# A pre-norm transformer block on one core: down projections of batches 1 to 3 as seven block products

## The chip, the cores and the metric

The kernel runs on 1 core of one Trainium2 chip. The metric is the device time of one execution in microseconds (us), as the median of several runs. The profile is one further execution, recorded by the hardware profiler. Everything is float32. Engines are named as in the profile: PE (TensorE, matrix multiplication), PEld (its weight loads), DVE (VectorE), ACT (ScalarE), POOL (GpSimd) and SP (SyncE, whose queue issues nearly all DMAs).

## The reference

The input holds 4 batches of 512 tokens with 512 features each. With `layernorm` the plain one without scale and shift, the block computes

```
x = x + attention(layernorm(x)) @ Wo        # 32 heads of 16, 8 key/value heads, rope, causal
h = layernorm(x)
x = x + (silu(h @ Wg.T) * (h @ Wu.T)) @ Wd.T    # hidden size 1376
```

The change concerns the last line's product with `Wd`, the down projection: per batch a matrix of 512 tokens by 1376 hidden features times a matrix of 1376 by 512, added to `x`.

## The kernel before

The kernel's program is written out by hand as lists of small steps with an estimated PE cost each. Attention is split in 32 groups (8 per batch, four heads each). While the 8 groups of a batch run, `slot(b, steps)` (L1017) deals steps of other work into the gaps between the attention's visits (`gap`, L1037, in proportion to the summed cost of the list). I call these stretches slot 0 to slot 3; what comes after slot 3 runs without attention beside it and is called the last section.

- Slot 1 holds the output projection of batch 0, its layer norm, its gate and up projections (`ordinary`, L507) and half of its down projection. It also packs combined gate and up weights into DRAM (`packs`, L585; POOL's L603).
- Slot 2 holds the other half of batch 0's down projection, then batch 1: `attended(1)` (output projection, residual add L478, layer norm statistics, and a transposition by DVE and two DMAs, `flipped`, L283, whose rows are called flips), `edge` (the hidden features from 1280 on), `seven` (gate and up projections as seven block products per pair of feature tiles, L647), and half of batch 1's down projection.
- Slot 3 is the same one batch further: rest of batch 1's down projection, batch 2's output projection, layer norm, `edge`, `seven`, and the beginning of its down projection.
- The last section holds the rest of batch 2's down projection and everything of batch 3.

`woven` (L1079) puts the output projection of the next batch (`before`) behind the first four leftover steps of a down projection, then the other leftover steps but one, then a step that emits the outstanding layer norm work (`behind`), then the last one.

The hidden features of a batch stand in `homes[n]` as 11 tiles of 128 features by 512 tokens, the last with 96 features. Tiles 0 to 9 are the `whole` ones. In `seven`, `ended` (L676) finishes a pair of tiles: two products of 128x512 on POOL inside a slot and on DVE outside (L684).

`down(b, n)` (L730) makes, for each of the four 128-token tiles of a batch, 11 products of a stationary 128x128 block of the hidden features with 512 columns of `wd_sb`, all accumulated in one PSUM bank. One DVE instruction (L740) scales by 0.5 and adds the bank to `xr`, and one DMA (L741) stores 256 KB. The down weights are read once into `wd_sb` (L1089). `xr` is a pool of six tiles of 128x512, loaded by L199.

`product_of` (L266) issues one product. Inside slots (`narrow`) it is split in four matmuls of 32 columns of the stationary block (L271); outside it is one matmul (L268). The profile counts each float32 matmul twice, so that a product is 8 records inside a slot and 2 outside. `bank()` (L190) hands out one of three PSUM banks. A list `aside` holds layer norm work that is emitted between steps, two entries per step in the last section.

The SP queue runs in order. Besides the loads of weights it carries what attention needs (`turned_round` L858, `laid_out` L867 and L869), the flips (L290, L292), and the stores of the output.

## Time and profile before

| | us |
|---|---|
| median of 3 runs (857.61 to 859.67) | 858.76 |
| the profiled execution, whole time | 859.25 |
| its span | 857.5 |
| PE busy | 836.6 |
| DVE busy | 533.9 |
| POOL busy | 292.1 |
| ACT busy | 217.1 |

The span is what the profile's times count from; the whole time is 1.7 us longer. Busy times are sums over the span, and the end of a matmul is modelled. Slot 2 ends at about 540 us, slot 3 at about 709 us, and the last section runs from there to the end. In it PE makes the rest of batch 2's down projection and batch 3's output projection (709.5 to 750.1), `edge` (to 755.4), `seven` (755.4 to 816.0) and batch 3's down projection (816.0 to 853.9).

### The profile page before, as it was taken

The page shows a single profiled execution, that of the slowest core. Times are in us where ns is not written, and L with a number is a line of the kernel's source. Part 1 is how long each engine was busy: PE and PEld are TensorE (multiplying, and loading weights), DVE is VectorE, ACT ScalarE, POOL GpSimd, SP SyncE. Part 2 cuts the span into 40 slices and gives each one's busy share as a digit, 9 for nine tenths or more (in the row PEclk, how much of TensorE's full clock was granted, in tenths as well). Part 3 has the DMA queues.
Part 4 walks back from the last instruction along what each step waited for, and adds up shares of the span by engine and source line. Part 5 has one row for each costly group of instructions (what it writes and reads, how often), then busy time and mean ns, then how long its engine had stood idle before and what let it go on. Part 6 is the DMA issues. An engine that isn't in the chain of part 4 may idle for free.

```text
span 857.5 us, 26970 instructions
## 1 busy us (share of the span) xinstructions
PE 836.6 (98%) x11446; PEld 420.5 (49%) x11446; DVE 533.9 (62%) x1593; ACT 217.1 (25%) x296; POOL 292.1 (34%) x418
## 2 busy tenths in 40 slices
PE   6999999999999999999999999999999999999998
PEld 5654453544333335333655553335555544498843
DVE  7887778878555554457777774586777523356610
ACT  1034444422222222221233332222333320011100
POOL 4565564773444344222233332232243330000000
PEclk9999999999999999999999999999999999999999
DMA  7533304003765742335134320214332402545300
GB/s 252 122 98 77 90 16 80 15 3 71 234 182 165 203 135 78 127 155 113 59 92 120 102 89 15 65 27 114 104 108 89 118 28 66 108 136 161 105 12 37
DMA packets 133463, 85.10 MB, mean 99 GB/s; under 512 B 59264, under 2 KB 120320, under 8 KB 133088
## 3 DMA queue, kind: packets, MB, share of 16 engines
q1 hardware_dynamic: 133056, 77.62, 32.4%
q10 hardware_dynamic: 288, 5.77, 1.7%
q8 instruction: 90, 1.47, 0.7%
q14 instruction: 29, 0.24, 0.1%
HBM read 64.56 MB, written 22.54 MB: 102 GB/s over the span
## 4 chain that ended last, share of the span: by engine, by line
PE 81%; DVE 10%; POOL 3%; DMA 2%; issue 2%; ACT 1%; SPq 1%; POOLq 0%; DVEq 0%; ACTq 0%
PE mm L271 38%; PE mm L268 18%; PE sc L771 12%; PE av L899 6%; DVE junk L817 6%; PE sc L784 4%; POOL e L877 2%; PE mm L553 2%; ACT e L872 1%; PE mm L545 1%; DVE st L218 1%; DVE rot L330 1%; DMA xa<-in_x 1%; POOL qa L756 1%; DMA shared<-in_wg 1%
## 5 line engine op out<-in xcount | busy, mean ns | idle before, releaser
L817 DVE CUSTOM_DVE_ANT_0 junk<-sc,mask 128x128 f32<-128x128 f32 (+3 forms) x512 | 251.0, 490 | 140.5 <-PE sc L784 80.3
L872 ACT ACTIVATE e<-sc 128x1024 f32<-128x1024 f32 (+1 forms) x192 | 165.4, 881 | 376.5 <-PE sc L784 307.8
L271 PE MATMUL mm<-xnT,shared 128*32 128x256 f32 (+1 forms) x3520 | 243.9, 420 | 1.4 <-DMA shared<-in_wg 1.4
L877 POOL TENSOR_SCALAR_AFFINE_SELECT e<-e 128x512 f32<-128x512 f32 (+2 forms) x192 | 106.2, 563 | 264.5 <-ACT e L872 261.3
L271 PEld LDWEIGHTS mm<-xnT,shared 128*32 128x32 f32 x3520 | 116.9, 110 | 112.1 <-issue 63.6
L771 PE MATMUL sc<-home,qa 32*64 32x512 f32 (+6 forms) x2048 | 157.9, 421 | 5.5 <-DVE low L817 3.1
L784 PE MATMUL sc<-qa,home 32*64 32x512 f32 (+6 forms) x2048 | 152.2, 427 | 2.2 <-DVE low L817 1.6
L771 PEld LDWEIGHTS sc<-home,qa 32*64 32x64 f32 x2048 | 67.3, 131 | 94.2 <-issue 31.1
L271 PE MATMUL mm<-wd_sb,home 128*32 128x512 f32 (+1 forms) x808 | 94.0, 595 | 0.0
L899 PE MATMUL av<-e,home 128*32 128x512 f32 (+3 forms) x1024 | 82.3, 437 | 1.5 <-POOL e L877 1.1
L268 PE MATMUL mm<-xnT,shared 128*128 128x256 f32 x360 | 80.6, 384 | 0.0
L268 PEld LDWEIGHTS mm<-xnT,shared 128*128 128x128 f32 x360 | 68.7, 192 | 11.7 <-issue 2.2
L784 PEld LDWEIGHTS sc<-qa,home 32*64 32x64 f32 x2048 | 58.7, 130 | 26.5 <-issue 8.7
L268 PE MATMUL mm<-wd_sb,home 128*128 128x512 f32 (+1 forms) x150 | 65.0, 593 | 0.0
L740 DVE SCALAR_TENSOR_TENSOR xr<-mm,xr 128x512 f32<-128x512 f32 x16 | 11.0, 686 | 71.5 <-PE mm L268 54.9
L899 PEld LDWEIGHTS av<-e,home 128*32 128x32 f32 x1024 | 30.9, 109 | 46.7 <-issue 35.5
L271 PEld LDWEIGHTS mm<-wd_sb,home 128*32 128x32 f32 (+1 forms) x808 | 26.9, 110 | 50.8 <-issue 48.9
L268 PEld LDWEIGHTS mm<-wd_sb,home 128*128 128x128 f32 (+1 forms) x150 | 28.4, 190 | 35.8 <-issue 35.8
L271 PE MATMUL mm<-wo_sb,cx 128*32 128x512 f32 x384 | 44.9, 595 | 0.0
L817 DVE DVE_READ_ACCUMULATOR2_ANT low<- 128x1 f32 x512 | 42.3, 83 | 0.0
L221 POOL TENSOR_TENSOR rstd<-rstd,neghalf 128x1 f32<-128x1 f32 x32 | 20.4, 639 | 61.4 <-DVE rstd L220 60.9
L923 POOL TENSOR_TENSOR inv<-us,inverse 128x256 f32<-128x256 f32 x32 | 20.9, 654 | 49.1 <-DVE inverse L916 47.9
(108 smaller groups left out, 669.5 us busy)
## 6 DMA issues: line engine op xcount, KB each, us to landing
shared<-packed SPq DMA_DIRECT2D x90, 256.0 KB
flip<-u SPq DMA_DIRECT2D x88, 64.0 KB
packed<-xnT SPq DMA_DIRECT2D x10, 512.0 KB
xnT<-flip SPq DMA_DIRECT2D x18, 256.0 KB
xr<-in_x SPq DMA_DIRECT2D x16, 256.0 KB
out<-xr SPq DMA_DIRECT2D x16, 256.0 KB
shared<-packed SPq DMA_DIRECT2D x30, 128.0 KB
xa<-in_x SPq DMA_DIRECT2D x12, 256.0 KB
```

Source lines behind the costliest of these rows:

```text
L221: nc.gpsimd.tensor_tensor(rstd, rstd, neghalf, ALU.pow)
L268: nc.tensor.matmul(out, lhsT=lhsT, rhs=rhs, start=start, stop=stop)
L271: nc.tensor.matmul(out[c : c + 32], lhsT=lhsT[:, c : c + 32], rhs=rhs, start=start, stop=stop)
L553: nc.tensor.matmul(ps[96:P, ts(q, P)], lhsT=rest_w[:, a, kq, 32 * q : 32 * q + 32], rhs=xnTs[0][:, kq, most:], start=kq == 0, stop=kq == N ...
L740: nc.vector.scalar_tensor_tensor(xr[b, i], py[i], 0.5, xr[b, i], ALU.mult, ALU.add)
L771: nc.tensor.matmul(dst[at : at + 64, :n], lhsT=qa[g][rows_of(r), q : q + 64], rhs=keys_of(g)[rows_of(r), :n], start=True, stop=True,)
L784: nc.tensor.matmul(dst[at : at + 64, first_q:], lhsT=keys_of(g)[rows_of(r), k : k + 64], rhs=qa[g][rows_of(r), P * j + first_q :], start=True,
L817: nc.vector.tensor_tensor_reduce(out=junk[:, :n], in0=src, in1=mask[:, T - n : T] if i else mask[:, T:], scale=-1.0, scalar=BIG, op0=ALU.a ...
L872: nc.scalar.activation(dst, src, AF.Exp, scale=1.0 / math.sqrt(DH))
L877: nc.gpsimd.affine_select(out=e[rows, heads, c : c + P], in_=e[rows, heads, c : c + P], compare_op=ALU.is_ge, fill=0.0, base=base, pattern ...
L899: nc.tensor.matmul(av[32 * r : 32 * r + 32, P * j :], lhsT=v[:, j, 4 * (m // 2) + r, DH * (1 - hf) : DH * (3 - hf)], rhs=e[:, r, c : c + n ...
L923: nc.gpsimd.tensor_tensor(us[m][:, :, hf, :], turned[0][:, :, hf, :], by, ALU.mult)
```

## The change

For batches 1 to 3 the ten whole feature tiles are taken as five pairs. For each pair, the hidden block (256 features by 512 tokens) and the weight block (256 features by 512 outputs) are cut into 2 by 2 blocks, and the product is made from seven block products instead of eight. Each of the seven products P1 to P7 is accumulated over the five pairs in a PSUM bank of its own, and DVE then adds the banks to the quadrants of the output. The 96 last features are multiplied as before, inside the banks of P2, P4 and P3 and in a bank called E.

- The combined hidden blocks are made by POOL (`hidden_sum`, four instructions of 128x256 per pair; two inside `seven`, two while P2 and P4 run).
- The combined weight blocks are made once by POOL in slot 2 (`differ`, 20 instructions) and stored to DRAM (five stores of 512 KB).
- The weight blocks of each stage are read as one DMA of 640 KB (`load_stage`), into places that stood free: two for batch 1, more for batches 2 and 3 (`PLACE`).
- `xr` becomes four fixed tiles of two rows each (`rows`).
- Per batch there are 39 steps of two products (256 columns each) instead of 20 steps; the first 17 stand where the first half stood, the next five where `woven` had four leftover steps, and the remaining 17 behind the output projection of the next batch.

```diff
-    xr = {}
+    rows = [const.tile([P, 2, D], F32, name=f"rows{n}") for n in range(3)] + [homes[3][:, 8:10, :]]
+    ROWS = {0: (0, 1), 1: (2, 0), 2: (1, 3), 3: (2, 0)}
+    xr = {(b, i): rows[ROWS[b][i // 2]][:, i % 2, :] for b in range(B) for i in range(NT)}
...
     def load_xr(b, i):
-        t = work.tile([P, D], F32, tag="xr", name="xr", bufs=6)
-        nc.sync.dma_start(out=t, in_=x[b, ts(i, P), :])
-        xr[b, i] = t
+        nc.sync.dma_start(out=xr[b, i], in_=x[b, ts(i, P), :])
...
-        steps = [step for u in range(whole) for step in unit(u)]
+        steps = []
+        for u in range(whole):
+            steps += unit(u)
+            for which in range(2 if u > 1 and u % 2 == 0 else 0):
+                steps.insert(len(steps) - 4 + 3 * which, after(lambda u=u, w=which: hidden_sum(n, u // 2 - 1, w)))
...
-        return [ends[0], t[0], ends[1], t[1], ends[2], t[2], ends[3], t[3], *steps[:12], after(moved), *steps[12:]]
+        last = [after(lambda w=w: hidden_sum(n, whole // 2 - 1, w)) for w in range(2)]
+        steps[12:12] = [after(moved)]
+        for cut, step in zip((44, 50, 56, 62, 66, 70), blocks):
+            steps.insert(cut, after(step))
+        return [ends[0], t[0], ends[1], t[1], ends[2], t[2], ends[3], t[3], *steps, *last]
...
+    def hidden_of(n, parity, half, p):
+        return homes[n][:, 2 * p + parity, halved_d * half : halved_d * (half + 1)]
+
+    def hidden_sum(n, p, which):
+        a11, a12, a21, a22 = (hidden_of(n, k, h, p) for h in range(2) for k in range(2))
+        s = third[:, p]
+        to, one, two, op = (
+            (s, a21, a22, ALU.add),
+            (a21, a11, a21, ALU.subtract),
+            (s, s, a11, ALU.subtract),
+            (a12, a12, s, ALU.subtract),
+        )[which]
+        nc.gpsimd.tensor_tensor(to, one, two, op)
+
+    def differ(p):
+        t = xnTs[1][:, 2 * (p % 2) : 2 * (p % 2) + 2, :].rearrange("p k t -> p (k t)")
+        t = t.rearrange("p (s d) -> p s d", s=4)
+        b11, b12, b21, b22 = (wd_sb[:, 2 * p + k, halved_d * h :][:, :halved_d] for k in range(2) for h in range(2))
+        def combine(which):
+            to, one, two = ((0, b12, b11), (1, b22, b12), (2, b22, t[:, 0]), (3, b21, t[:, 2]))[which]
+            nc.gpsimd.tensor_tensor(t[:, to], one, two, ALU.subtract)
+        def store():
+            nc.sync.dma_start(out=differences[:, p], in_=t)
...
+    STAGES = (("P5", None, 0), ("P2", (0, 0), (1, 0)), ("P4", (1, 0), 3), ("P7", None, 1),
+        ("P1", None, (0, 0)), ("P6", None, 2), ("E", (1, 1), None), ("P3", (0, 1), (1, 1)))
+    PLACE = {1: (0, 1, 0, 1, 0, 1, 0), 2: (1, 0, 1, 0, 2, 3, 4), 3: (5, 0, 1, 2, 3, 4, 5)}
...
+        lefts = {
+            "P5": lambda p: third[:, p],
+            "P6": lambda p: third[:, p],
+            "P2": lambda p: hidden_of(n, 1, 0, p),
+            "P3": lambda p: hidden_of(n, 1, 0, p),
+            "P1": lambda p: hidden_of(n, 0, 0, p),
+            "P7": lambda p: hidden_of(n, 0, 1, p),
+            "P4": lambda p: hidden_of(n, 1, 1, p),
+        }
...
+        def add(half, d, name):
+            at = quadrant(half, d)
+            nc.vector.scalar_tensor_tensor(at, two(banks[name]), 0.5, at, ALU.mult, ALU.add)
...
+        ends = {
+            "P5": [lambda: add(0, 1, "P5"), lambda: add(1, 1, "P5")],
+            "P2": [lambda: add(0, 0, "P2")],
+            "P4": [lambda: add(1, 0, "P4")],
+            "P7": [lambda: add(1, 0, "P7"), lambda: add(1, 1, "P7")],
+            "P1": [keep, lambda: final(0, 0, "P1")],
+            "P6": [joined, lambda: final(1, 0, "P6"), lambda: add(1, 1, "P6"), lambda: add(0, 1, "P6")],
+            "E": [lambda: final(1, 1, "E")],
+            "P3": [lambda: final(0, 1, "P3")] if b < B - 1 else [],
+        }
...
+            inner = [*(range(5) if name != "E" else ()), *([None] if edge else ())]
+            todo = [(i, p, p == inner[0], p == inner[-1]) for i in range(2) for p in inner]
...
+                steps.append((0.86, lambda args=args: step(*args)))
+                if at == 0 and k is not None and (b == 1 and 1 <= k < 6 or b == 2 and 1 <= k < 3):
+                    steps.append(after(lambda k=k: load_stage(b, k + 1)))
+                if at == 0 and name == "P2" and b == 3:
+                    steps.append(after(lambda: load_stage(3, 6)))
+                if name in ("P2", "P4") and at < 10:
+                    which = 2 if name == "P2" else 3
+                    steps.append(after(lambda p=at // 2, which=which: hidden_sum(n, p, which)))
...
+    asides = []
+    for p in range(5):
+        combine, store = differ(p)
+        asides += [(0.5 + 5.2 * p + 1.2 * n, lambda n=n, combine=combine: combine(n)) for n in range(4)]
+        asides += [(7.0 + 5.2 * p, store)]
...
-    slot(2, [after(restored), *woven(before, others, behind), *seven(1, 0), *tiles[:cut]])
+    opening = timed([*others[:4], *before, *others[4:-1], *behind, others[-1]], asides)
+    now, opener, rest = split(1, 0)
+    slot(2, [after(restored), *opening, *seven(1, 0, stages_of(1, (0, 1))), *now])
...
-    slot(3, [*woven(before, others, behind), *seven(2, 2), *tiles[:cut]])
+    woven = [*opener, *before, *rest[:-1], *behind, rest[-1]]
+    now, opener, rest = split(2, 2)
+    slot(3, [*woven, *seven(2, 2, stages_of(2, (0, 1))), *now])
...
-    for cost, step in [*woven(before, tiles[cut:], behind), *seven(3, 0), *down(3, 0)]:
+    loads = [after(step) for step in stages_of(2, (4, 5, 6))]
+    woven = [*opener, *loads, *before, *rest[:-1], *behind, rest[-1]]
+    for cost, step in [*woven, *seven(3, 0, stages_of(3, range(6))), *down7(3, 0)]:
```

In `step` (inside `down7`, not shown) each step first emits one of the DVE additions that the stages before it owe, then its two products; those of P4, P7 and P3 are emitted at the end of the stage. `keep` is two ACT copies of P1's bank, `joined` two DVE additions of 128x256, `final` an addition and a store of 256 KB. P3 of batch 3 is added and stored by 128x256 halves.

More of the change, by code (lines that the diff above doesn't have):

```diff
@@ L491, in begin @@
         def begin():
-            if (b, 0) not in xr:
+            if b > 0:
                 for i in range(NT):
@@ L645, in sums_of, with seven @@
         nc.vector.tensor_tensor(one, two, by, ALU.subtract)
-    def seven(b, n):
+    def seven(b, n, blocks):
         x, home = xnTs[0], homes[n]
@@ new lines, in seven @@
+        steps[12:12] = [after(moved)]
+        for cut, step in zip((44, 50, 56, 62, 66, 70), blocks):
+            steps.insert(cut, after(step))
+        return [ends[0], t[0], ends[1], t[1], ends[2], t[2], ends[3], t[3], *steps, *last]
+    halved_d = 2 * P
+    pieces = homes[3].rearrange("p f t -> p (f t)")[:, : 8 * T]
+    ring = [pieces[:, 1280 * s : 1280 * (s + 1)] for s in range(2)]
+    ring += [homes[1].rearrange("p f t -> p (f t)")[:, 1280 * s : 1280 * (s + 1)] for s in range(4)]
+    ring = [t.rearrange("p (j d) -> p j d", j=5) for t in ring]
@@ new lines, in preln_block_kernel @@
+    third = pieces[:, 2560 : 2560 + 1280].rearrange("p (j t) -> p j t", j=5)
+    differences = dram.tile([P, 5, 4, halved_d], F32, name="differences")
+    def hidden_of(n, parity, half, p):
[10 more added lines that the diff above has]
+        nc.gpsimd.tensor_tensor(to, one, two, op)
@@ new lines, in differ @@
+    def differ(p):
[7 more added lines that the diff above has]
+            nc.sync.dma_start(out=differences[:, p], in_=t)
+        return combine, store
@@ new lines, in preln_block_kernel, with load_stage @@
+    STAGES = (
+        ("P5", None, 0),
+        ("P2", (0, 0), (1, 0)),
+        ("P4", (1, 0), 3),
+        ("P7", None, 1),
+        ("P1", None, (0, 0)),
+        ("P6", None, 2),
+        ("E", (1, 1), None),
+        ("P3", (0, 1), (1, 1)),
+    )
+    NAMES = [name for name, _, _ in STAGES if name != "E"]
+    PLACE = {1: (0, 1, 0, 1, 0, 1, 0), 2: (1, 0, 1, 0, 2, 3, 4), 3: (5, 0, 1, 2, 3, 4, 5)}
+    def load_stage(b, k):
+        src = next(src for name, _, src in STAGES if name == NAMES[k])
+        if isinstance(src, int):
+            view = differences[:, :, src, :]
+        else:
+            parity, half = src
+            view = wd[: whole * P, halved_d * half : halved_d * (half + 1)]
+            view = view.rearrange("(j a p) d -> a p j d", a=2, p=P)[parity]
+        nc.sync.dma_start(out=ring[PLACE[b][k]], in_=view)
@@ new lines, in down7, with quadrant, two, give @@
+    def down7(b, n):
+        banks, owed, steps = {}, deque(), []
+        lefts = {
[7 more added lines that the diff above has]
+        }
+        def quadrant(half, d):
+            return rows[ROWS[b][half]][:, :, halved_d * d : halved_d * (d + 1)]
+        def two(t):
+            return t.rearrange("p (i d) -> p i d", i=2)
+        def add(half, d, name):
+            at = quadrant(half, d)
+            nc.vector.scalar_tensor_tensor(at, two(banks[name]), 0.5, at, ALU.mult, ALU.add)
+        def give(half, d):
+            to = out[b, halved_d * half : halved_d * (half + 1), halved_d * d : halved_d * (d + 1)]
+            nc.sync.dma_start(out=to.rearrange("(i p) d -> p i d", p=P), in_=quadrant(half, d))
+        kept = (rope_sb[:, 2 * NK * 96 : 2 * T], pieces[:, 15 * halved_d :])
+        def keep():
+            for i in range(2):
+                nc.scalar.copy(kept[i], banks["P1"][:, ts(i, halved_d)])
+        def joined():
+            for i in range(2):
+                at = banks["P6"][:, ts(i, halved_d)]
+                nc.vector.tensor_tensor(at, at, kept[i], ALU.add)
+        def final(half, d, name):
+            add(half, d, name)
+            give(half, d)
+        ends = {
[8 more added lines that the diff above has]
+        }
+        def product(name, i, left, right, first, last):
+            product_of(banks[name][:, ts(i, halved_d)], left[:, ts(i, P)], right, first, last)
+        def step(name, products, first, final_step):
+            if first:
+                banks[name] = bank()
+            if owed:
+                owed.popleft()()
+            for i, p, start, stop in products:
+                if p is None:
+                    half, d = edges[name]
+                    left = homes[n][: FF - whole * P, whole, halved_d * half : halved_d * (half + 1)]
+                    right = wd_sb[: FF - whole * P, whole, halved_d * d : halved_d * (d + 1)]
+                else:
+                    left, right = lefts[name](p), ring[PLACE[b][NAMES.index(name)]][:, p]
+                product(name, i, left, right, start, stop)
+                if stop and b == B - 1 and name == "P3":
+                    at = quadrant(0, 1)[:, i]
+                    nc.vector.scalar_tensor_tensor(at, two(banks[name])[:, i], 0.5, at, ALU.mult, ALU.add)
+                    nc.sync.dma_start(out=out[b, ts(i, P), halved_d:], in_=at)
+            if final_step:
+                owed.extend(ends[name])
+                while owed and (name in ("P4", "P7", "P3") or owed[0] in (keep, joined)):
+                    owed.popleft()()
+        edges = {name: edge for name, edge, _ in STAGES}
+        for name, edge, _ in STAGES:
+            inner = [*(range(5) if name != "E" else ()), *([None] if edge else ())]
+            todo = [(i, p, p == inner[0], p == inner[-1]) for i in range(2) for p in inner]
+            k = NAMES.index(name) if name != "E" else None
+            for at in range(0, len(todo), 2):
+                args = name, todo[at : at + 2], at == 0, at + 2 == len(todo)
+                steps.append((0.86, lambda args=args: step(*args)))
[6 more added lines that the diff above has]
+                    steps.append(after(lambda p=at // 2, which=which: hidden_sum(n, p, which)))
+        return steps
@@ L1077, in slot @@
             step()
-    def woven(before, others, behind):
-        return [*others[:4], *before, *others[4:-1], *behind, others[-1]]
     def spilled():
@@ L1138, in preln_block_kernel, with split, stages_of @@
     slot(1, [*start1, *timed(layer, asides)])
+    asides = []
[3 more added lines that the diff above has]
+        asides += [(7.0 + 5.2 * p, store)]
+    def split(b, n):
+        steps = down7(b, n)
+        at = [[i for i, (cost, _) in enumerate(steps) if cost][k] for k in (17, 22)]
+        return steps[: at[0]], steps[at[0] : at[1]], steps[at[1] :]
+    def stages_of(b, ks):
+        return [lambda k=k: load_stage(b, k) for k in ks]
     before, behind = attended(1)
-    tiles, others = list(down(1, 0)), tiles[cut:]
-    cut = len(tiles) // 2
-    slot(2, [after(restored), *woven(before, others, behind), *seven(1, 0), *tiles[:cut]])
+    others = tiles[cut:]
+    opening = timed([*others[:4], *before, *others[4:-1], *behind, others[-1]], asides)
+    now, opener, rest = split(1, 0)
+    slot(2, [after(restored), *opening, *seven(1, 0, stages_of(1, (0, 1))), *now])
     before, behind = attended(2)
-    tiles, others = list(down(2, 2)), tiles[cut:]
-    cut -= 4
-    slot(3, [*woven(before, others, behind), *seven(2, 2), *tiles[:cut]])
+    woven = [*opener, *before, *rest[:-1], *behind, rest[-1]]
+    now, opener, rest = split(2, 2)
+    slot(3, [*woven, *seven(2, 2, stages_of(2, (0, 1))), *now])
     before, behind = attended(3)
-    for cost, step in [*woven(before, tiles[cut:], behind), *seven(3, 0), *down(3, 0)]:
+    loads = [after(step) for step in stages_of(2, (4, 5, 6))]
+    woven = [*opener, *loads, *before, *rest[:-1], *behind, rest[-1]]
+    for cost, step in [*woven, *seven(3, 0, stages_of(3, range(6))), *down7(3, 0)]:
         step()
```

## The prediction

> **What bounds the kernel now.** I read the page first: its busy times, the granted clock and the chain that ended last.

> ```profile
> PE 836.6 (98%) x11446; PEld 420.5 (49%) x11446; DVE 533.9 (62%) x1593; ACT 217.1 (25%) x296; POOL 292.1 (34%) x418
> ...
> PEclk9999999999999999999999999999999999999999
> ...
> PE 81%; DVE 10%; POOL 3%; DMA 2%; issue 2%; ACT 1%; SPq 1%; POOLq 0%; DVEq 0%; ACTq 0%
> ```

> PE is busy 98% of the span at full clock and carries 81% of the chain. Of PE's 21 us of idle time all but about 1 lie in the first 215 us and behind its last matmul (the table of windows). So in the stretches that the change touches, PE time taken away is time won, and a wait of PE is time lost.

> Second, the groups with shapes kept apart, for counts and for POOL's prices.

> ```profile
> L271 PE MATMUL mm<-wd_sb,home 128*32 128x512 f32 x736 | 86.4, 595 | 0.0
> ...
> L268 PE MATMUL mm<-wd_sb,home 128*128 128x512 f32 x136 | 59.6, 593 | 0.0
> ...
> L603 POOL TENSOR_TENSOR xnT<-xnT 128x256 f32<-128x256 f32 x40 | 29.2, 731 | 4.9 <-DMA xnT<-in_wg 2.1 <-DMA xnT<-in_wu 0.7
> ...
> L684 POOL TENSOR_TENSOR home<-home,u 128x512 f32<-128x512 f32 x20 | 25.2, 1283 | 24.8 <-DVE u L720 24.6
> ...
> L740 DVE SCALAR_TENSOR_TENSOR xr<-mm,xr 128x512 f32<-128x512 f32 x16 | 11.0, 686 | 71.5 <-PE mm L268 54.9 <-PE mm L271 16.6
> ```

> The means overlap each other in pipelined matmuls, so they are no price. For that I took bursts from the timeline of PE (start, length, count):

> ```profile
> 508.95 1.93 PE L271 MATMUL mm<-xnT,shared 128*32 128x256 f32 x32
> ...
> 657.77 3.66 PE L271 MATMUL mm<-xnT,shared 128*32 128x256 f32 x64
> ...
> 567.07 3.64 PE L271 MATMUL mm<-wo_sb,cx 128*32 128x512 f32 x32
> 571.58 1.92 PE L271 MATMUL mm<-wo_sb,cx 128*32 128x512 f32 x16
> ...
> 764.83 51.32 PE L268 MATMUL mm<-xnT,shared 128*128 128x256 f32 x237
> 815.98 37.95 PE L268 MATMUL mm<-wd_sb,home 128*128 128x512 f32 x88
> ```

> In a slot 16 more records of 512 columns (two products) take 1.72 us, so 0.86 a product; 32 more of 256 columns (four products) take 1.73, so 0.4325. In the last section it is 37.95/44 = 0.8625 and 51.32 x 2/237 = 0.433. Half the columns cost half: smaller products are not punished, though each needs a weight load of its own.

> **The change, part by part.** *Matmuls.* Before, batches 1 and 2 have 44 + 13 products of 512 columns in slots, and 31 + 44 stand in the last section. After, 78 + 34 of 256 columns stand in slots, and 44 + 78 in the last section. Slots: 57 x 0.86 = 49.0 against 112 x 0.4325 = 48.4. Last section: 75 x 0.8625 = 64.7 against 122 x 0.433 = 52.8. Sum: -12.5 us. Nearly all of it appears in the last section, since 17 of 39 steps stand in slot 3 where 6 of 20 did.

> *The end.* The last instructions before:

> ```profile
> 816.18 0.69 DVE L720 TENSOR_TENSOR u<-mm,u 128x512 f32<-128x512 f32 x1 [0.58 <-PE mm L268]
> 816.91 1.29 DVE L684 TENSOR_TENSOR home<-home,u 128x512 f32<-128x512 f32 x2
> ...
> 853.96 0.69 DVE L740 SCALAR_TENSOR_TENSOR xr<-mm,xr 128x512 f32<-128x512 f32 x1 [8.76 <-PE mm L268]
> ```

> The last addition becomes 128x256 (0.42, row of L712), and its store 128 KB instead of 256: at the 320 GB/s of the busiest slices 0.4 us less. Together -0.6 (0 to -0.8).

> *The wait for the combined hidden block.* The first two lines above also price the hand-over. P5 begins where tile 0 of the down projection began, but its fifth product needs the sum of the two blocks that the last unit of `seven` has just finished; before, those tiles were the ninth and tenth of eleven, 6.9 us in. Batch 3: from the last matmul of `seven` (816.0) DVE needs until 818.2, POOL's sum 0.73 and hand-overs 0.2, so the block is ready after 3.1 us. PE has four products until then, 1.7 us: it waits 1.4. Batches 1 and 2: both products of L684 run on POOL (2.5 us), behind L720, which DVE reaches 0.2 us late behind its transposition; ready after 0.9 + 2.5 + 0.8 + 0.2 = 4.4 us. In the order that the changed program is built in, PE has two products (0.87), one visit of scores (1.0) and two products (0.87) meanwhile: it waits 1.6 each. Sum +4.6 (0, if other work lies between, to 6, if POOL is late by one select of 0.64 each time).

> *Batch 1's blocks in slot 3.* Batch 1 has two places in turn, so P3's block can only be read when P1 is done, and the read is queued on SP behind everything that the output projection of batch 2 triggers. SP before, there:

> ```profile
> 578.94 2.09 SPq L290 DMA_DIRECT2D flip<-u  x4
> ...
> 584.55 3.90 SPq L292 DMA_DIRECT2D xnT<-flip  x2
> ...
> 718.66 1.97 SPq L199 DMA_DIRECT2D xr<-in_x  x4
> ```

> The output projection ended on PE at 573.5; call it O. The last transposed read left SP at 588.4, O + 15, since it waits for flips to land. A read of 256 KB issued at 718.66 had its reader start at 721.62: 2.1 us besides 0.8 of data, so 640 KB take 4.2. After, P1 starts at O; 22 products (9.5 us), two visits (0.95 each) and the last visit with its averages (3.4) come before P3, at O + 14.8. Its read leaves at about O + 14.4 (the flips come 0.6 earlier in the new order) and lands at O + 18.6: PE waits 3.8 in all. Part of this shows earlier: P6's read, behind the flips of tile 1, lands 1 to 3 us late; and DVE, busy 17.9 of the 20 us from 560, has more layer norm work ahead of a visit's minima in the new order and holds that visit. These don't add up; they move P3, whose time the read sets. Between 0 (flips leave 4 us earlier) and 7 (the read meets the 0.85 busy DMA slices that stood at 580 to 588): 3.8, nearest to the rows.

> *Slot 2's opening.* 20 POOL instructions (0.73 each) and five stores; slot 1 has 40 of the same and ten stores, and PE idles 0.3 us in its last 100 us. But the fifth store is queued behind `laid_out`, and the sums of `seven` (L645) overwrite what it reads: DVE may wait up to 2 us there, with 0.3 us of slack to PE. +0.6 (0 to 2).

> *Reads in the last seven.* Six reads of 640 KB fall in about 22 us that already move 132 GB/s, so 307 GB/s against the 320 seen: +0.4 (0 to 2.5, one landing late by the backlog).

> *The rest.* Eight more DVE additions (0.69) and two of 0.42 per batch, two ACT copies (0.36), 40 POOL sums inside slots: beside PE. DVE has 5 us in 20 free from 600 on; without that cover a batch costs 6.4 us. The averages' weight loads already wait up to 0.9 us for POOL's selects, hidden by the matmuls before them: +0.2 (0 to 2). `rows` has the same reuse distances as the pool of six: 0.

> [...]

> Sum: -12.5 - 0.6 + 4.6 + 3.8 + 0.6 + 0.4 + 0.2 = -3.5. The profiled execution took 859.25, span plus 1.7, and lies 0.5 above the median of 858.76. 859.25 - 3.5 = 855.75, on the median's footing **855.3**.

> **The rivals.** (B) *The waits are covered:* the steps are dealt by cost, so P5's fifth product may fall behind a visit, and flips may leave sooner. For it: PE hardly waits anywhere in slots 2 and 3 now. Against: the built order puts only 2.75 us of PE work ahead of the block. With 2 us left of the 8.4, 849.

> (C) *Slower, through the block reads:* the seven reads inside slots 2 and 3 become PE's bound. The slack of the earliest, P4's, is 7.1 us of stage less 4.2. If SP or DMA makes each three us later (the 3.9 us line is such a delay), P4 of both batches, P6 and P3 lose together 6 us more: 861.3. It decides from 9 us of PE waiting on block reads. Against: the slots move about 100 GB/s on average.

> [...]

> That the change doesn't shorten PE's work is excluded by the counts and by the price of half columns.

> **How the numbers follow.** Chances: forecast (852.5 to 857.5) 0.47, B 0.23, C 0.17, D 0.13. The range takes in B's 849 and most of C: 849 to 861.5; the likeliest alone has 852.5 to 857.5. About 0.2%, 1.7 us, is what a measurement of this kernel can tell from no change, so faster means below 857.0. Faster: 0.42 of the first and B, 0.65; same: the rest of the first and D, 0.17; slower: C and a little of D, 0.18.

> **What the profile after would show.** In the last section the down projections have 244 matmul records of 256 columns where 150 of 512 stood, and the stretch from slot 3's end to the end is about 10.5 us shorter. Right: three waits of a P5 product for POOL's sum, 1.4 to 1.6 us each; PE waiting for the DMA of a weight block near P3 of batch 1. Wrong: no such waits (B), the same on P4 and P7 (C), or L817 as the releaser of long PE waits from 550 to 590 (D). The forecast fails most easily in slot 3's opening, where three queues meet.

## The result and the profile after

| | before | after |
|---|---|---|
| median of 10 runs | 858.60 us (857.61 to 859.67) | 861.36 us (859.79 to 862.69) |
| ratio after/before | | 1.003, 95% interval 1.002 to 1.004 |
| profiled execution, its own time | 859.25 us | 860.13 us |
| span | 857.5 us | 858.4 us |

The change made the kernel slower by 2.8 us, where 3.5 us of gain were forecast. The range of 849.0 to 861.5 just holds the median; the direction was wrong. The profiled execution is one of the shorter ones of the changed kernel, so its span shows 0.9 us of the 2.8.

The page of the changed kernel, the lines that answer to those shown of before (engines with busy time and instruction counts; granted PE clock in 40 slices; the chain that ended last):

```profile
PE 827.8 (96%) x11980; PEld 452.3 (53%) x11980; DVE 554.0 (65%) x1624; ACT 218.9 (25%) x302; POOL 348.1 (41%) x498
...
PEclk9999999999999999999999999999999999999999
...
PE 73%; DVE 14%; POOL 4%; DMA 4%; issue 2%; ACT 2%; SPq 1%; POOLq 0%; DVEq 0%; ACTq 0%
```

PE is busy 8.8 us less, but the span is longer: PE's idle time grew from 20.9 to 30.6 us, and the chain runs 73% over PE instead of 81%. The row of the clock (the granted clock is the share of its full speed that PE is given) looks full. Its digits hide the dip that the text comes to below.

The waits of PE from 400 us on (in total, times, longest). Before, this stretch had two waits, of 0.4 and 0.3 us:

```profile
PE mm L271 <- DMA wd_sb<-differences: 3.1, 1, 3.1
PE mm L271 <- POOL wd_sb L760: 2.7, 2, 1.4
PE av L1066 <- POOL e L1044: 2.3, 4, 1.6
PE mm L268 <- POOL wd_sb L760: 1.2, 1, 1.2
PE mm L271 <- DVE mm L838: 0.7, 1, 0.7
PE mm L268 <- DVE rows L873: 0.5, 1, 0.5
```

L760 is the combined hidden block that P5 waits for, forecast; the first line is P6's block of batch 1; L1044 is a causal select on POOL that the averages wait for; L838 is the sum of P1 and P6; L873 is the addition of the first half of batch 3's P3, which holds the bank that PE wants for the second half. The same waits in the timeline of PE, with the burst that each one holds:

```profile
402.20 0.77 PE L1066 MATMUL av<-e,home 128*32 128x256 f32 x6 [1.64 <-POOL e L1044]
...
521.01 1.93 PE L271 MATMUL mm<-wd_sb 128*32 128x256 f32 x32 [1.44 <-POOL wd_sb L760]
...
579.54 5.04 PE L271 MATMUL mm<-wd_sb 128*32 128x256 f32 x64 [3.09 <-DMA wd_sb<-differences]
...
590.28 1.07 PE L271 MATMUL mm<-wd_sb,home 128*32 128x256 f32 x16 [0.66 <-DVE mm L838]
...
720.14 4.58 PE L268 MATMUL mm<-wd_sb,home 128*128 128x256 f32 x20
...
758.46 60.70 PE L268 MATMUL mm<-xnT,shared 128*128 128x256 f32 x280
...
822.13 2.86 PE L268 MATMUL mm<-home,wd_sb 128*128 128x256 f32 x12 [1.25 <-POOL wd_sb L760]
```

The last section begins at 720.14 (709.52 before) and its last matmul ends at 855.2 (853.9 before): 9.4 us shorter, and 9.7 to the end of the span, where 10.5 were forecast. So the last section did nearly what was said of it, and slot 3 alone gave it back: at slot 2's last averages (535.80; 536.17 before) the program is 0.4 us early, at slot 3's second (585.45; 579.96) 5.5 and at its last (715.21; 705.46) 9.8 us late. Of these 10.2 us, from 0.4 early to 9.8 late, some 3.5 are work that the change moved into slot 3 and 5.0 the waits shown there (3.09, 0.66 and 1.29, the last at batch 2's P5); most of the rest is the slower clock that comes next.

The burst at 579.54 holds a cost that the prediction doesn't have. Its 64 records took 5.04 us; 64 such records took 3.66 in the profile of before. The table of windows over L271, with the granted clock (behind the PE and PEld columns):

```profile
574.00:576.00 2.00, 1.38 (x28) 0.55 (x20) 1.00 0.92 275
576.00:578.00 2.00, 0.00 (x0) 0.00 (x0) 1.00 1.14 273
578.00:580.00 2.00, 0.46 (x8) 0.29 (x12) 0.74 0.28 51
580.00:582.00 2.00, 2.00 (x24) 1.08 (x20) 0.50 0.89 196
582.00:584.00 2.00, 2.00 (x40) 1.22 (x36) 0.90 0.87 194
```

The clock is halved for (0.26 + 0.5 + 0.1) x 2 x 2 = 3.4 us. The first window holds 1.0 of them, and P6 ran for only 0.5 of that window, so about 0.6 us of the half clock lie in the wait itself and cost nothing; the other 2.8 cost 1.4, which is what the burst took longer (5.04 - 3.66). The block itself waited in SP's queue (SP's timeline):

```profile
573.40 0.57 SPq L799 DMA_DIRECT2D wd_sb<-differences  x1
574.07 3.82 SPq L290 DMA_DIRECT2D flip<-u  x4
...
583.97 0.50 SPq L827 DMA_DIRECT2D out<-rows  x1
584.57 0.41 SPq L799 DMA_DIRECT2D wd_sb<-in_wd  x1
```

P6's block left SP at 573.40, after the flips of tile 1, and PE got it at 579.5: 6.1 us for 640 KB, where 4.2 were forecast; the window behind its issue moved 273 GB/s at a DMA share of 1.14. P3's block left at 584.57, behind the last transposed tiles.

### The profile page after: what moved, and what is told of

Read it like the earlier page. It is cut to its first block, busy times and chain, and to the rows that moved or that the text cites. A ratio compares the mean times of both kernels' runs of the same rounds, so it can differ in the third digit from the quotient of the medians.

```text
span 858.4 us, 28211 instructions
## 1 busy us (share of the span) xinstructions
PE 827.8 (96%) x11980; PEld 452.3 (53%) x11980; DVE 554.0 (65%) x1624; ACT 218.9 (25%) x302; POOL 348.1 (41%) x498
## 4 chain that ended last, share of the span: by engine, by line
PE 73%; DVE 14%; POOL 4%; DMA 4%; issue 2%; ACT 2%; SPq 1%; POOLq 0%; DVEq 0%; ACTq 0%
PE mm L271 36%; PE mm L268 15%; PE sc L938 11%; DVE junk L984 7%; PE av L1066 5%; PE sc L951 3%; POOL e L1044 2%; PE mm L553 2%; ACT e L1039 1%; DVE st L218 1%; PE mm L545 1%; DVE rot L330 1%; SPq L290 1%; DMA wd_sb<-differences 1%; DVE u L286 1%
## 5 line engine op out<-in xcount | busy, mean ns | idle before, releaser
L984 DVE CUSTOM_DVE_ANT_0 junk<-sc,mask 128x128 f32<-128x128 f32 (+3 forms) x512 | 250.8, 490 | 139.9 <-PE sc L951 81.1
L271 PE MATMUL mm<-xnT,shared 128*32 128x256 f32 (+1 forms) x3520 | 243.9, 420 | 1.1 <-DMA shared<-in_wg 1.1
L1044 POOL TENSOR_SCALAR_AFFINE_SELECT e<-e 128x512 f32<-128x512 f32 (+2 forms) x192 | 105.5, 560 | 227.0 <-ACT e L1039 223.6
L271 PEld LDWEIGHTS mm<-xnT,shared 128*32 128x32 f32 x3520 | 116.4, 110 | 111.9 <-issue 60.8
L271 PE MATMUL mm<-wd_sb,home 128*32 128x256 f32 (+3 forms) x1008 | 80.2, 455 | 0.7 <-DVE mm L838 0.7
L268 PE MATMUL mm<-xnT,shared 128*128 128x256 f32 x360 | 80.1, 383 | 0.0
L268 PEld LDWEIGHTS mm<-xnT,shared 128*128 128x128 f32 x360 | 68.4, 192 | 11.6 <-issue 2.2
L951 PEld LDWEIGHTS sc<-qa,home 32*64 32x64 f32 x2048 | 58.8, 130 | 24.8 <-issue 8.7
L271 PEld LDWEIGHTS mm<-wd_sb,home 128*32 128x32 f32 (+1 forms) x1008 | 34.2, 110 | 38.4 <-issue 25.9
L221 POOL TENSOR_TENSOR rstd<-rstd,neghalf 128x1 f32<-128x1 f32 x32 | 20.9, 653 | 65.5 <-DVE rstd L220 65.3
L271 PE MATMUL mm<-wo_sb,cx 128*32 128x512 f32 x384 | 45.6, 595 | 0.0
L984 DVE DVE_READ_ACCUMULATOR2_ANT low<- 128x1 f32 x512 | 42.2, 82 | 0.0
L823 DVE SCALAR_TENSOR_TENSOR rows<-mm,rows 128x512 f32<-128x512 f32 x28 | 18.4, 685 | 36.3 <-PE mm L268 18.5
L760 POOL TENSOR_TENSOR wd_sb<-home 128x256 f32<-128x256 f32 x15 | 10.9, 726 | 74.7 <-DVE home L684 74.0
L331 POOL TENSOR_TENSOR rot<-rot,rope_sb 128x512 f32<-128x512 f32 x18 | 26.6, 1479 | 28.0 <-DVE rot L330 27.8
```

The source lines that it names most:

```text
L221: nc.gpsimd.tensor_tensor(rstd, rstd, neghalf, ALU.pow)
L268: nc.tensor.matmul(out, lhsT=lhsT, rhs=rhs, start=start, stop=stop)
L271: nc.tensor.matmul(out[c : c + 32], lhsT=lhsT[:, c : c + 32], rhs=rhs, start=start, stop=stop)
L331: put(lambda: engine.tensor_tensor(rot, rot, sin, ALU.mult))
L823: nc.vector.scalar_tensor_tensor(at, two(banks[name]), 0.5, at, ALU.mult, ALU.add)
L951: nc.tensor.matmul(dst[at : at + 64, first_q:], lhsT=keys_of(g)[rows_of(r), k : k + 64], rhs=qa[g][rows_of(r), P * j + first_q :], start=True,
```

## The experiments

All runs were compared with runs of the kernel before on the same chip, whose median was 858.6 to 859.5; I give differences to that. On this footing the changed kernel stands at +2.8.

| run | edit | median, us | ratio to before, 95% | difference, us |
|---|---|---|---|---|
| e1 | batch 1's P1 and both late reads ahead of the output projection | 859.92 | 0.9997 to 1.0015 | +0.7 |
| e2 | P1 first | 861.31 | 1.0012 to 1.0039 | +2.1 |
| e3 | differences of the weights in `seven` | 861.22 | 1.0011 to 1.0030 | +2.0 |
| e4 | all three | 852.52 | 0.9905 to 0.9930 | -6.7 |
| e5 | P6's read alone earlier | 861.99 | 1.0023 to 1.0050 | +2.8 |
| e6 | e4 mended | 847.87 | 0.9856 to 0.9882 | -11.3 |
| e7 | differences behind the averages | 859.66 | 0.9991 to 1.0012 | +0.5 |
| e8 | e6 without P1 first | 854.27 | 0.9933 to 0.9964 | -4.9 |
| e9 | PE kept busy ahead of P6 | 864.98 | 1.0047 to 1.0075 | +5.4 |
| e10 | e6, last hidden tiles on DVE | 848.36 | 0.9852 to 0.9888 | -11.2 |

**e1: the late reads.**

```diff
-  ... (b == 1 and 1 <= k < 6 or b == 2 and 1 <= k < 3)
+  ... (b == 1 and 1 <= k < 5 or b == 2 and 1 <= k < 3)
-  ... for k in (17, 22)]
+  ... for k in ((17, 27) if b == 1 else (17, 22))]
-    woven = [*opener, *before, *rest[:-1], *behind, rest[-1]]
+    late = [after(step) for step in stages_of(1, (6,))]
+    woven = [*opener, *late, *before, *rest[:-1], *behind, rest[-1]]
```

> Only batch 1 changes: its P1 moves ahead of the output projection of batch 2, beside P7, so that both places of its ring are free there and the blocks of P6 and P3 are read before the transposed tiles of batch 2 queue up on SP. Against 861.4 us of the changed kernel. Theory (late reads): PE's wait of 3.1 us for P6's block goes, with it the 3.4 us at half clock behind it (1.7 us lost) and the 0.7 us wait for the joined sum (L838): 861.4 - 5.5 = 855.9 (855.0 to 857.5), and the granted clock has no 0.50 before the end. Rival (the layer norm of batch 2 sets the pace of slot 3's opening): 24 products instead of 34 stand behind the output projection, PE reaches the edge tile sooner and waits there for the transposed tiles instead: 859.5 to 861.5.

2.1 us of the 5.5 came, which is a time of the rival's range. In the profiled execution the clock stayed at 1.00 from 560 to 600, P6 and P3 waited for nothing, and PE did not wait for transposed tiles: the rival's mechanism fell. But two new waits stood ahead of the output projection. P1's block was wanted at 547.4 and had left SP at 545.18 (a wait of 1.7), and P3's read, which waits for P1's end, stood in SP ahead of batch 2's rows. SP's, POOL's and PE's timelines:

```profile
554.82 0.38 SPq L799 DMA_DIRECT2D wd_sb<-in_wd  x1
555.25 2.45 SPq L200 DMA_DIRECT2D rows<-in_x  x2
```

```profile
562.80 0.55 POOL L221 TENSOR_TENSOR rstd<-rstd,neghalf 128x1 f32<-128x1 f32 x1 [3.88 <-DVE rstd L220]
563.32 0.77 POOL L1044 TENSOR_SCALAR_AFFINE_SELECT e<-e 128x256 f32<-128x256 f32 x2
```

```profile
563.78 0.77 PE L1066 MATMUL av<-e,home 128*32 128x256 f32 x6 [1.71 <-POOL e L1044]
```

The rows left SP at 555.25 behind the read; DVE could add to them only at 560.83; POOL's root of the variance waited for DVE, the select stood behind that root, and the averages behind the select. One read ahead of another cost PE 1.7 us, 9 us later and over three engines. In e8 below, where the rows leave SP first (at 546.28), these averages wait 0.22 us; in e4, where the read stands ahead of the rows as here, no such wait shows either; why it doesn't is open.

**e2: the hand-over to POOL's sum.**

```diff
     STAGES = (
+        ("P1", None, (0, 0)),
         ("P5", None, 0),
...
-        ("P1", None, (0, 0)),
-            "P2": [lambda: add(0, 0, "P2")],
+            "P2": [lambda: final(0, 0, "P2")],
-            "P1": [keep, lambda: final(0, 0, "P1")],
+            "P1": [keep, lambda: add(0, 0, "P1")],
```

> Only the order of the seven stages changes: P1, which needs no combined block, goes first in all three batches, then P5. Theory (hand-over to POOL's sum): the three waits of P5's fifth product (1.44, 1.29 and 1.25 us) go and nothing takes their place, since 10 products or 4.3 us lie ahead of P5 and P1's own last block is ready 0.7 us sooner than the sum: 861.4 - 4.0 = 857.4 (856.5 to 858.5); the wait for P6's block and the half clock stay. Rival (DVE behind seven's end): PE waits at P1's fifth product, or at P5's first for the bank that ACT's copy still holds, for about as long: 860 to 861.4.

The three waits of P5 went; 0.48, 0.50 and 0.39 us for the last hidden tiles (L684) came. Yet the median moved by 0.7 us. In PE's timeline:

```profile
584.88 5.35 PE L271 MATMUL mm<-wd_sb 128*32 128x256 f32 x48 [7.25 <-DMA wd_sb<-differences]
```

Its table of windows over L271:

```profile
578.00:582.00 4.00, 0.00 (x0) 0.00 (x0) 0.82 0.66 138
582.00:586.00 4.00, 1.12 (x12) 0.69 (x16) 0.50 0.91 225
586.00:590.00 4.00, 4.00 (x40) 1.84 (x32) 0.50 0.81 227
590.00:594.00 4.00, 0.66 (x12) 0.64 (x12) 0.90 0.18 53
```

P6's block was issued at 579.83, one transposed tile later than in the changed kernel. The wait grew from 3.1 to 7.2 us and the half clock from 3.4 to 10.2. (This profiled execution, 863.9 us, is a long one for the kernel; nine of the twelve have a mean clock of 0.996, so some 6.8 us of half clock.) What P5 gave, P6 took: an edit ahead of slot 3's opening shortens the program only as far as it brings this read forward too.

**e3 and e7: POOL ahead of the selects.** e3 moved the 20 subtractions into the `seven` of slot 2 through two other buffers; e7 put them, four at a time, directly behind a group's averages:

```diff
-        asides += [(0.5 + 5.2 * p + 1.2 * n, lambda n=n, combine=combine: combine(n)) for n in range(4)]
-        asides += [(7.0 + 5.2 * p, store)]
+        between.extend([*(lambda n=n, combine=combine: combine(n) for n in range(4)), store])
...
             averages(g)
+            for _ in range(min(5, len(between))):
+                between.popleft()()
```

> Only the 20 POOL subtractions that make the four differences of the down weights move, from slot 2's opening into its seven-product stretch, through two other buffers. Theory (POOL in front of the selects): in slot 2's opening the averages no longer wait 1.64 us for a select behind four subtractions, and two waits of 0.4 us for minima go: 861.4 - 2.2 = 859.2 (858.3 to 860.3), with up to 1 us of selects late in the stretch that takes them. Rival (the opening is held by SP's five stores between the transposed tiles, or by DVE): the opening loses the same 3.4 us against the kernel before, and the time is 861 to 862.

> The changed kernel (861.4 us) with this one edit alone: the 20 subtractions stand behind the averages of slot 2 instead of in its opening. Theory: the wait of 1.6 us for a select goes and none takes its place in slot 2, so 859.8 (858.8 to 860.6). Rival (slot 3's opening takes it back, as its block reads come when they come): 860.6 to 862, with PE waiting longer for P6's or P3's block.

What e7 removed stands in POOL's timeline of the changed kernel, four subtractions between the selects of one group:

```profile
398.87 1.43 POOL L771 TENSOR_TENSOR xnT<-wd_sb 128x256 f32<-128x256 f32 x2
400.25 1.53 POOL L771 TENSOR_TENSOR xnT<-wd_sb,xnT 128x256 f32<-128x256 f32 x2
401.74 0.76 POOL L1044 TENSOR_SCALAR_AFFINE_SELECT e<-e 128x256 f32<-128x256 f32 x2
```

In both runs the wait of 1.6 us in the opening went, so the rival that SP's stores or DVE hold the opening fell. Of the two waits of 0.4 us for minima one fell to 0.2, the other stayed at 0.39: that one isn't due to the subtractions, and its cause is open. e3 gained 0.8 us and e7 2.3, although P3's block then waited in both (2.2 and 3.1 us, where the changed kernel has 0.7). The placing of e3 has its own price, a wait of 1.30 us for a select in e3 and of 2.30 us in e4, behind three subtractions and a sum in the stretch that took them:

```profile
446.43 0.77 PE L1073 MATMUL av<-e,home 128*32 128x256 f32 x6 [2.30 <-POOL e L1051]
```

**e5: one read alone.**

```diff
-  ... (b == 1 and 1 <= k < 6 or b == 2 and 1 <= k < 3)
+  ... (b == 1 and k in (1, 2, 3, 5) or b == 2 and 1 <= k < 3)
-    woven = [*opener, *before, *rest[:-1], *behind, rest[-1]]
+    late = [after(step) for step in stages_of(1, (5,))]
+    woven = [*opener, before[0], *late, *before[1:], *rest[:-1], *behind, rest[-1]]
```

> One read is moved: batch 1's block for P6 is queued on SP before the output projection of batch 2, where its place is already free, instead of between the transposed tiles. Everything else is the changed kernel (861.4 us). Theory (the place in SP's queue): PE's wait of 3.1 us for this block goes, and with it 1.7 us of half clock and the 0.7 us for the joined sum; but P3's block, whose place is free only when P1 is done, still leaves SP at about 584.5 of the profile and lands at 588.5, and PE now comes to it some 4 us sooner: a wait of about 3 us takes the place, 861.4 - 5.5 + 3 = 858.9 (857.5 to 860.3). Rival (the slot is bound by other work there, the waits only mark it): 860.8 to 862.

PE's timeline of e5, P6 and then P3:

```profile
577.91 3.66 PE L271 MATMUL mm<-wd_sb 128*32 128x256 f32 x64
...
590.28 1.07 PE L271 MATMUL mm<-wd_sb,home 128*32 128x256 f32 x16 [3.67 <-DMA wd_sb<-in_wd]
593.22 3.52 PE L271 MATMUL mm<-wd_sb,home 128*32 128x256 f32 x48
```

P6 ran at once and at full clock. P3's block left SP at 585.21 (584.5 expected) and PE waited 3.7 us for it (3 expected), but the half clock went with the wait: the 48 records behind it took 3.52 us instead of 2.80. The net is nothing, as the rival had it, for the reason of the theory: two reads behind the flips, and the second one takes over what the first gave.

**e9: the half clock.** Six useless products are put ahead of P6, so that PE has the same block to wait for, but not idle:

```diff
+            if first and b == 1 and name == "P6":
+                for p in (0, 1, 2, 3, 4, 0):
+                    product(name, 0, hidden_of(n, 0, 0, p), ring[0][:, p], True, True)
```

> The changed kernel with six useless products (2.6 us of PE at 0.4325) ahead of batch 1's P6, into the bank that P6's first product then starts afresh. PE has the same block to wait for, but is idle for about 0.5 us there instead of 3.1. Theory (the idle time itself brings the half clock): no stretch of half clock in slot 3's opening, so P6's eight products take 3.7 us instead of 5.0 and the time falls although PE has more to do: by 1.2 to 1.7 us, on the footing of the kernel before 0.5 to 1.5 us above it instead of 2.8. Rival (the half clock comes from something else at that place, from DMA load or from the start of P6): the row of 0.50 stays and the time is unchanged or up to 1 us longer.

PE's timeline of e9, the six products (48 records), P6, and P3:

```profile
576.58 2.80 PE L271 MATMUL mm<-wd_sb,home 128*32 128x256 f32 x48
580.02 3.66 PE L271 MATMUL mm<-wd_sb 128*32 128x256 f32 x64 [0.64 <-DMA wd_sb<-differences]
...
592.04 1.94 PE L271 MATMUL mm<-wd_sb,home 128*32 128x256 f32 x16 [3.32 <-DMA wd_sb<-in_wd]
```

The block came at nearly the same point (within 0.5 us), and with 0.64 us of idle time instead of 3.09 P6's products took 3.66 us instead of 5.04: at the same place, and with the DMA engines as busy behind the read (share 1.12 from 576 to 578, 1.14 in the changed kernel), the half clock came with the long idle time and not with the short one. The total was not gained; it was lost at P3. Its block left SP at 586.26 (584.57 in the changed kernel), PE idled 3.3 us for it, and the clock was halved for 6.8 us from about the last 1.0 us of that wait on.

**e4, e6, e8, e10: the versions together.** e4 holds the edits of e1 and e2 (with P4 and P7 ahead of the output projection), that of e3, and a bank of its own for each half of batch 3's P3. e6 takes e7's placing instead of e3's and queues the rows ahead of the late read (`before[0], *late`). e8 is e6 with P5 first. e10 is e6 with L684 of the last unit on DVE (`narrow[0] and u < whole - 1`).

> All three edits, with batch 1's P4 and P7 ahead of the output projection, and the two halves of batch 3's last stage (P3) in banks of their own, so that PE doesn't wait 0.5 us for the first half's addition. Theory (the waits are separate and add up): 861.4 - 5.5 - 4.0 - 2.2 - 0.5 = 849.2 (847.5 to 851.5), faster than the kernel before by about 1.1%. Rival (the waits hide each other, and DVE or the layer norm chain comes next): 854 to 858.

> The version with all edits (852.5 us), but the POOL subtractions of the down weights stand directly behind a group's averages in slot 2, four at a time, where no select is due for some us, and batch 2's residual rows are queued on SP ahead of the late block read. Theory (what costs is a subtraction in front of a select): the waits of 2.3 and 0.5 us for selects that the averages had in slot 2 go: 852.5 - 2.8 = 849.7 (848.5 to 851.2). Rival (POOL has too little free time in slot 2, wherever they stand): 852 to 853.5.

> The mended version with the old order of stages (P5 first), all else kept: P7 and P1 stand ahead of batch 2's output projection. Theory (P5's waits cost their own length once nothing else waits): against the mended version + 1.44 + 1.29 + 1.25 for P5's waits, - 0.48 - 0.50 - 0.39 for the waits that the other order has in their place, and + 1.7 if P1's block again lands late: 2.6 to 4.3 us above it, so 852.3 to 854. Rival (the waits are hidden by other slack): within 1 us of it.

> The mended version (847.9 us), with the last unit's two products of hidden tiles (L684) on DVE instead of POOL in slots 2 and 3 as well. Theory (P1's last block waits for POOL): the two waits of 0.48 and 0.50 us go, 846.9 (846.2 to 847.6). Rival (DVE is the later engine there): no change, or up to 1 us longer.

The page and PE's waits from 400 us on of e6:

```profile
PE 824.6 (97%) x11968; PEld 454.1 (54%) x11968; DVE 552.4 (65%) x1624; ACT 219.0 (26%) x302; POOL 348.3 (41%) x498
...
PE 81%; DVE 11%; POOL 4%; issue 2%; DMA 1%; ACT 1%; POOLq 0%; DVEq 0%; ACTq 0%
```

```profile
PE mm L271 <- POOL home L684: 1.0, 2, 0.5
PE mm L268 <- DVE home L684: 0.4, 1, 0.4
PE av L1073 <- POOL e L1051: 0.2, 1, 0.2
PE sc L958 <- DVE low L991: 0.2, 1, 0.2
```

e6 is 1.3% faster than the kernel before and 1.6% faster than the changed one. No block read holds PE, the clock is full, and PE's busy time is 836.6 - 824.6 = 12.0 us below that of before: the term of -12.5 was there all along. e4 lacked 2.7 us of its expected 9.4, for which the wait of 2.3 us above is the largest named cause; e6 gained 4.6 over it where 2.8 were expected. The spans of the profiled executions lie 2.7 apart, as the two waits for selects (2.30 and 0.49) say; the rest of the 4.6 is open. e8 stands 6.4 us above e6 in the medians, more than the 2.6 to 4.3 expected, and 5.0 in the profiles; named waits explain 4.3 (its 1.46, 1.30 and 1.25 for POOL's sum, 1.24 for P1's block and 0.7 for selects, less 1.6 in e6). Why the medians differ by 2 us more than the named waits is open. Alone P1 first was worth 0.7 us (e2), with the reads mended 6.4, of which 4.3 are named: the wait at the read had hidden it. In e10 the two waits of 0.5 us on POOL went and the median stayed; its profiled execution waits 1.8 us for a block of packed gate weights in the last `seven` instead.

## Why the prediction was wrong

- *Matmuls, -12.5:* right. 12.0 us of PE busy time in e6; in the changed kernel the rest of batch 2's products went from 40.55 to 32.94 us with the output projection between them, 7.6 of the 7.7 forecast.
- *Wait for the combined hidden block, 1.6, 1.6 and 1.4:* right in place and size: 1.44, 1.29 and 1.25, in all 4.0 instead of 4.6.
- *Batch 1's blocks in slot 3, +3.8:* the first of two steps that failed. The mechanism was right (SP, behind the flips), and where P6 is fed early its forecast is met closely: P1 begins at 571.46 in e5 and P3 at 590.28, O + 18.8, where O + 18.6 was said (the read left SP 0.6 us earlier than said and took 5.1 us instead of 4.2). But the step let P6's read land only 1 to 3 us late and be absorbed in P3's. It took 6.1 us instead of 4.2 and cost 3.1 us itself, so that P3 stood at O + 20.5 and waited for no block. That the waits alone, 3.1 + 0.7 (L838), come to the forecast's 3.8 is luck. And the step knew waits only as idle time: the half clock at this wait is 1.4 us more. Together 3.1 + 1.4 + 0.7 = 5.2.
- *Slot 2's opening, +0.6 (0 to 2):* the second step that failed, and the larger error: 1.6 us and two waits of 0.4, in all 2.4. The step looked at the fifth store and the sums of `seven`. What cost most was POOL's order: four subtractions of 0.73 us ahead of one group's last select. Slot 1's 40 were no measure, since it matters where they fall between the selects. e7's median shows 2.3 us for it, though the waits that went there are only 1.8.
- *Not in the sum:* 0.5 us for the two halves of batch 3's P3 in one bank.
- *The end, -0.6, and the reads in the last seven, +0.4:* -0.3 (from the last matmul to the end of the span 3.6, then 3.2 us), and 0: `seven` takes 60.5 us in both. e3 and e10 show waits of 0.2 and 1.8 there, so the bound of 2.5 was fair.
- *DVE beside POOL,* no term of the sum: L681 at 489.59 us took 1.24 us, beside a hidden sum on POOL from 489.55 on, where 0.69 is usual, and its 30 instructions took 23.1 us instead of 21.0. (Before, two of them took 0.98.) It isn't seen as a term of PE's time: all named waits above have other causes, and in e6, with as many POOL instructions (498, busy for 348.3 us, 348.1 in the changed kernel), PE was as busy as forecast. No run varied it alone, so what lengthens these instructions isn't shown.

The errors: +1.4 at the block reads, +1.8 in the opening, +0.5 for the half banks, +0.5 and +0.3 at the matmuls and the end, less 0.6 at P5 and 0.4 in the last `seven`: from -3.5 to 0.0. The profiled execution has +0.9; the difference is open, but it isn't waiting: PE's busy time fell by 8.8 us, where e6's 12.0 less 1.4 for the half clock would be 10.6. The other 1.9 us to the medians' +2.8 lie between executions: those of the changed kernel reach from 859.8 to 862.7, and the two longest show a mean granted clock of 0.996 where the others show 0.998, which is one more stretch of 3.4 us at half clock. That such stretches and the landing of two reads make the rest is argued, not shown.

Of the rivals, C came out in time (861.3 against 861.4), not in mechanism: P4's reads made no wait in either batch, and PE's waits on block reads were 3.1 us, not 9. B was excluded by the three waits at P5. D's sign, DVE's L984 (L817 before) as the releaser of long PE waits in slot 3's opening, didn't come: PE's one wait from 550 to 590 beyond 0.3 us is the 3.09 us for P6's block. No run shows what DVE's work beside POOL's costs in time; what slot 2's opening showed is another thing, the order of POOL's own work.

## What to carry to other kernels

Before adding transfers to a queue that already carries a dependency chain, list for each transfer what stands ahead of it there and when that can leave: in e5 an earlier place in the queue took away P6's wait of 3.1 us, and P3's read, which left SP when it did before (585.21 against 584.57), brought one of 3.7. In these runs a PE wait of 3.1 to 3.7 us cost more than its length: 1.7 us for each stretch of 3.4 us at half clock, less half of what of it fell into the wait, so 1.4 us more in the changed kernel (3.09) and 1.7 in e5 (3.67); the 3.3 us of e9 brought 6.8 us at half clock. When an edit that removes a proven wait gains nothing, look for the next event with a time of its own behind it (here a read in SP's queue): the edits of e1, e2 and e3 were worth 2.1, 0.7 and 0.8 us one at a time, and 9.5 together with the half banks.
